# Values gathered in one tile and stored once per head, keys of two heads stored together, and projection weights split one row tile earlier

## The chip, the cores and the metric

The kernel runs on one core of a Trainium2 chip. The core has five engines with an instruction stream each: TensorE (PE in the profile, with its weight loads as PEld), VectorE (DVE), ScalarE (ACT), GpSimd (POOL) and SyncE (SP, which here only issues DMAs). Each stream runs in order; streams wait for each other through semaphores. DMAs move data between SBUF, where the engines work, and DRAM. The metric is the device time of one execution in microseconds; lower is better. The figure to compare is the median of several executions.

## The reference

```python
xn = layernorm(x)                                  # x: 1024 rows x 512
q = rmsnorm(xn @ Wq.T, q_norm_w)                   # 32 heads of 128
k = rmsnorm(xn @ Wk.T, k_norm_w)                   # 8 heads of 128
v = xn @ Wv.T                                      # 8 heads of 128
scores = q k^T / sqrt(128) + alibi bias, causal    # 4 query heads share one key/value head
s = (softmax(scores) @ v) @ Wo.T
g = silu(down(silu(xn @ gate) * (xn @ up)))        # weights dequantized from integers, width 1792
out = x + s * g
```

All inputs and the output are float32 (the quantized weights are integers).

## The kernel before

The work comes in four stages. First the layer norm, whose result is kept transposed as a high and a low float16 part (`xth`, `xtl`). Then the gate and up projections and the down projection of the feed-forward part, whose result is parked in DRAM (`gd`). Then the projections of queries, keys and values, which go through DRAM as well. Last the attention with its output projection, which ends with the output.

The change lies in the third stage and in the end of the second. There are 12 projections of 512 columns (line 618): in turn one of kind `kv` (keys and values of two heads, 256 + 256 columns) and two of kind `q` (four query heads each). Each is computed in 8 row tiles of 128 rows. A row tile is 12 matmuls of 512 columns (`mm3`: high by high, high by low, low by high, for four parts of the inner size) into one PSUM tile. The PSUM tiles take turns over two tags with two buffers each, so TensorE can be at most four row tiles ahead of the engines that empty them.

`Projection.tile` (line 532) issues a row tile's matmuls and the work that empties it. On ScalarE: a copy to `f` (542), squares with sums for the norm (544), and for `kv` the high part of the values (548). On VectorE for `kv`: the low part of the values (549). Both parts go to `v16`, a small tile with three buffers (546), and `store_values` (552) stores them one step later with two DMAs, one for each head.

The queries and keys are finished later, through a table of deferred work, `finishing`, which `finish_step` (448) runs once per row tile (`defer`, and `queue_half` at line 715). The steps are the inverse norm on VectorE (`inverse`) and GpSimd (`newton`), the multiplication on GpSimd (`normalize`), the high and low halves on VectorE (`halves`, 592), a DMA transpose (`transposed`, 606) one step after that and the store (`store`, 611) two steps after that. The finishing of a projection thus mostly falls into the next projection. While a `kv` projection runs, the finishing of a `q` projection goes on beside it.

The weights of projection k+1 are prepared during projection k by `prepare` (623), at given row tiles t: at t = 0 `squares` (471, sums of squares of the weight columns, on ScalarE), at 2 `norms` (483, a small matmul and scale factors on VectorE), at 3 `scale`, at 6 `factors`, and at 3 to 6 the split into high and low parts, `wh` on ScalarE (523) and `wl` on VectorE (524); for `kv` two head parts and then two value parts. The raw weights come by four DMAs in row tiles 0 to 3 of projection k-1 (line 966), into a pool of two buffers.

The order on every engine is the order in which the loop at lines 957 to 975 issues the work: in a row tile `prepare` for the next projection, the load for the one after that, the row tile itself, then the deferred work. All DMAs of the stage are issued by SP, in that order: weight loads (469), value stores (554), DMA transposes (608), query stores (613), key stores (616). Before the tenth projection the first keys, values and queries of the attention are loaded, and in the last two projections every second row tile also issues a step of the attention.

In DRAM the keys lie in one buffer per head, `kd` (124), row tile by row tile with 512 bytes per partition, and the values in one buffer per head, `vd` (125), partition by partition. `load_keys` (738) and `load_values` (742) bring a whole head back for the attention.

Of the kernel before, what the change touches and what calls it, by code (L numbers as in the profile page):

```python
# [12 lines left out]
F16 = mybir.dt.float16  # L13
# [8 lines left out]
P = 128  # L22
# [3 lines left out]
HKV = 8  # L26
NH = 4
HD = 128
FF = 1792
NI = FF // P  # L30
NT = S // P
# [39 lines left out]
def attention_gated_by_ffn_kernel(ctx, tc, x, gu_w, gu_z, gu_s, dn_w, dn_z, dn_s, wq, wkv, wo, qnw, knw, out):  # L71
    nc = tc.nc
    ve, se, ge, te, sp = nc.vector, nc.scalar, nc.gpsimd, nc.tensor, nc.sync

    const = ctx.enter_context(tc.tile_pool(name="const", bufs=1))
    dram = ctx.enter_context(tc.tile_pool(name="scratch", bufs=1, space=DRAM))
# [5 lines left out]
    def ps1(tag, name):  # L82
        return psum[0].tile([P, 512], F32, tag=tag, name=name)
# [22 lines left out]
    def mm3(ps, lhs, rhs, first, last):  # L106
        (lh, ll), (rh, rl) = lhs, rhs
        te.matmul(ps, lhsT=lh, rhs=rh, start=first, stop=False)  # L108
        te.matmul(ps, lhsT=lh, rhs=rl, start=False, stop=False)  # L109
        te.matmul(ps, lhsT=ll, rhs=rh, start=False, stop=last)  # L110
# [10 lines left out]
    eps = const.tile([P, 3 * HKV // 2, NH], F32, name="eps")  # L121
    gsT = const.tile([P, NI, 2, KT], F32, name="gsT")

    kd = [dram.tile([NT, P, 2 * HD], F16, name=f"kd{g}") for g in range(HKV)]
    vd = [dram.tile([P, NT, 2 * HD], F16, name=f"vd{g}") for g in range(HKV)]
    qd = [dram.tile([NT, P, 2 * NH * HD], F16, name=f"qd{g}") for g in range(HKV)]
    ald = [dram.tile([1, 2 * HD], F32, name=f"ald{i}") for i in range(HKV // 2)]
# [2 lines left out]
    left = ExitStack()  # L130
# [3 lines left out]
    wp = left.enter_context(tc.tile_pool(name="w", bufs=1))  # L134
# [264 lines left out]
    def dn_load(it):  # L399
        if it % 2 == 0:  # L400
            wi = gp.tile([P, 2, DM], I32, tag="wi", name=f"dni{it}", bufs=3)
            sp.dma_start(wi, dn_w[it * P : (it + 2) * P, :].rearrange("(t p) c -> p t c", p=P))
            dn_raw["pair"] = (wi, wi.bitcast(F32))
        zi = gp.tile([P, DM], I32, tag="dzi", name=f"dnz{it}")
        si = gp.tile([P, DM], F32, tag="dsi", name=f"dns{it}")
        sp.dma_start(zi, dn_z[it].partition_broadcast(P))
        sp.dma_start(si, dn_s[it].partition_broadcast(P))
        dn_raw[it] = tuple(w[:, it % 2, :] for w in dn_raw["pair"]) + (zi, si)

    def dn_dequant(it, engine=ge):  # L410
        wi, wf, zi, si = dn_raw[it]
        ve.tensor_tensor(wf, wi, zi, ALU.subtract)
        engine.tensor_tensor(wf, wf, si, ALU.mult)
# [40 lines left out]
    def defer(steps, f):  # L454
        finishing.setdefault(clock[0] + steps, []).append(f)
# [4 lines left out]
    class Projection:  # L460
# [71 lines left out]
        def tile(self, t):  # L532
            n, half, r = self.n, t // HT, t % HT
            if r == 0:
                self.f[half] = fq.tile([P, HT, n, HD], F32, tag="f", name=f"f_{self.name}_{half}", bufs=3)
                self.ss[half] = fq.tile([P, HT, n], F32, tag="ss", name=f"ss_{self.name}_{half}", bufs=3)
                self.jk = wp.tile([P, NH, HD], BF16, tag="jk", name=f"jk_{self.name}_{half}")
            ps = ps1("o" if t % 2 else "m", f"ps_{self.name}_{t}")
            rows = slice(t * P, (t + 1) * P)
            for j in range(KT):  # L540
                mm3(ps, (xth[:, j, rows], xtl[:, j, rows]), (self.wh[:, j, :], self.wl[:, j, :]), j == 0, j == KT - 1)
            se.copy(self.f[half][:, r], ps[:, : n * HD].rearrange("p (g d) -> p g d", g=n))
            for i in range(n):
                se.activation(self.jk[:, i], ps[:, i * HD : (i + 1) * HD], AF.Square, accum_out=self.ss[half][:, r, i : i + 1])
            if self.kind == "kv":
                v16 = wp.tile([P, 2, 2, HD], F16, tag="v16", name=f"v16_{self.i}_{t}", bufs=3)
                vp = ps[:, 256:512].rearrange("p (g d) -> p g d", g=2)
                se.copy(v16[:, :, 0, :], vp)
                ve.tensor_tensor(v16[:, :, 1, :], vp, v16[:, :, 0, :], ALU.subtract)
                defer(1, lambda: self.store_values(t, v16))  # L550

        def store_values(self, t, v16):
            for i in range(2):
                sp.dma_start(vd[2 * self.i + i][:, t, :], v16[:, i].rearrange("p a d -> p (a d)"))

        def inverse(self, half):

# [53 lines left out]
        def store(self, t, tr):  # L611
            if self.kind == "q":
                sp.dma_start(qd[self.i][t], tr.rearrange("p c t -> p (c t)"))
            else:
                for i in range(2):
                    sp.dma_start(kd[2 * self.i + i][t], tr[:, 2 * i : 2 * i + 2].rearrange("p c t -> p (c t)"))

    projections = []
    for pr in range(HKV // 2):
# [3 lines left out]
    def prepare(k, t):  # L623

        if k < len(projections):
            p = projections[k]
            if t == 0:
                p.squares()
            elif t == 2:
                p.norms()  # L630
            elif t == 3:
                p.scale()
            elif t == 6:
                p.factors()
            if 3 <= t < 3 + p.n:
                p.split_head(t - 3)
            elif p.kind == "kv" and 5 <= t < 7:
                p.split_values(t - 5)

    def down_begin():  # L640
        dn_split_w(0)
# [4 lines left out]
    for it in range(3, NI):  # L646
        if it < 3 + 2 * KT:
            projections[(it - 3) // KT].load((it - 3) % KT)
        last = it == NI - 1
        gu_unit(  # L650
            it,
            None,
            it + 1 if not last else None,
            meanwhile={NI - 2: lambda: dn_dequant(0, ve), NI - 1: down_begin}.get(it, lambda: None),
            total=not last,
        )
        if it == NI - 5:
            prepare(0, 0)
        if it == NI - 4:
            prepare(0, 2)  # L660
        if it == NI - 3:
            dn_load(0)
            dn_load(1)
        if last:
            dn_load(2)
            dn_split_h(0, 1)
# [3 lines left out]
    for it in range(NI):  # L670
        for tb in range(2):
            if it == 0:
                two = [pair(f"dn_ps{tb}_{i}") for i in range(2)]
                acc[tb] = [two[i // 2][:, i % 2, :] for i in range(4)]
            if tb == 0:
                if it + 2 < NI:
                    dn_dequant(it + 2)
                if it + 3 < NI:
                    dn_load(it + 3)
                if it + 1 < NI:  # L680
                    dn_split_w(it + 1)
            if it + 1 < NI:
                dn_split_h(it + 1, tb)
            wh, wl = dn_w_hl[it]
            hh, hl = dn_h_hl.pop((it, tb))
            for i in range(4):
                c = slice(i * P, i * P + P)
                mm3(acc[tb][i], (hh[:, c], hl[:, c]), (wh, wl), it == 0, it == NI - 1)
            if tb:
                if it in (1, 2):  # L690
                    gu_total((NI - 1, None), it - 1)
                elif it == 3:
                    gu_finish(0)
                elif it == 4:
                    gu_finish(1)
                elif it == 5:
                    norm_weights()
                elif it >= NI - 6:
                    prepare(0, 9 - NI + it)
            if it == NI - 1:  # L700
                for i in range(4):
                    go = h[:, i, tb * 512 : tb * 512 + 512]
                    se.activation(go, acc[tb][i], AF.Silu)
                    sp.dma_start(gd[tb * 4 + i], go)
    ffn.close()
    psum.append(ctx.enter_context(tc.tile_pool(name="psum", bufs=2, space=PSUM)))


    fq = ctx.enter_context(tc.tile_pool(name="finish", bufs=2, side="right"))
    ap1 = ctx.enter_context(tc.tile_pool(name="attn1", bufs=2, side="right"))  # L710
    nrel = ap1.tile([P, S], F32, name="nrel", bufs=1)
# [23 lines left out]
    kT, vT, qT, woh, wol = {}, {}, {}, {}, {}  # L735
    trel, pT, oT, wor = {}, {}, {}, {}

    def load_keys(g):
        kT[g] = ap1.tile([P, NT, 2, P], F16, tag="kT", name=f"kT{g}")
        sp.dma_start(kT[g].rearrange("p t a k -> p t (a k)"), kd[g].rearrange("t p c -> p t c"))  # L740

    def load_values(g):
        vT[g] = ap1.tile([P, NT, 2, HD], F16, tag="vT", name=f"vT{g}")
# [213 lines left out]
    for k, p in enumerate(projections):  # L957
        if k == len(projections) - 3:
            load_keys(0)
            load_values(0)  # L960
            load_queries(*blocks[0])
            relative(0)
        for t in range(NT):
            prepare(k + 1, t)
            if k + 2 < len(projections) and t < KT:
                projections[k + 2].load(t)
            if t == HT:
                p.undo()
            p.tile(t)
            finish_step()  # L970
            if t % HT == HT - 1:
                queue_half(p, t // HT)
            if k >= len(projections) - 2 and t % 2 == 0:
                step(early)
                early += 1
# [46 lines left out]
```

## Time and profile before

| what | value |
| --- | --- |
| median of 3 executions | 1104.58 us (1102.62 to 1104.69) |
| the profiled execution | 1104.1 us, span 1102.3 us |
| PE busy in the span | 1029.0 us (93%) |
| DVE, ACT, POOL busy | 885.0, 794.4, 392.9 us |
| projections of q, k, v | 221.00 to 504.00 us |
| DMA queue of SP | 196.93 MB, 81.5% of 16 engines |

The span is the time between the first and the last instruction of the program in the profiled execution. "Busy" is the time in which an engine executes an instruction; matmuls overlap, so a busy TensorE is not necessarily at its peak. An engine's idle time is put down to what ended it. The issue of a DMA is an instruction of SP; the transfer itself comes after it and is told as a time to landing. The granted clock is the share of TensorE's full clock that it ran at.

### The profile page before, as it was taken

The page shows a single profiled execution, that of the slowest core. Times are in us where ns is not written, and L with a number is a line of the kernel's source. Part 1 is how long each engine was busy: PE and PEld are TensorE (multiplying, and loading weights), DVE is VectorE, ACT ScalarE, POOL GpSimd, SP SyncE. Part 2 cuts the span into 40 slices and gives each one's busy share as a digit, 9 for nine tenths or more (in the row PEclk, how much of TensorE's full clock was granted, in tenths as well). Part 3 has the DMA queues.
Part 4 walks back from the last instruction along what each step waited for, and adds up shares of the span by engine and source line. Part 5 has one row for each costly group of instructions (what it writes and reads, how often), then busy time and mean ns, then how long its engine had stood idle before and what let it go on. Part 6 is the DMA issues. An engine that isn't in the chain of part 4 may idle for free.

```text
span 1102.3 us, 18743 instructions
## 1 busy us (share of the span) xinstructions
PE 1029.0 (93%) x5912; PEld 623.2 (57%) x5912; DVE 885.0 (80%) x1752; ACT 794.4 (72%) x2123; POOL 392.9 (36%) x545
## 2 busy tenths in 40 slices
PE   7899899999999899898899999999999999999996
PEld 5333368844434344344666666666666576676664
DVE  7888897537787776787789797898898887969984
ACT  5767543478678585787789687797896887868972
POOL 2565552136878678560202304014021030033122
PEclk8999999999999999899999999999999999999999
DMA  5123245246998979979989999999997997999995
GB/s 195 58 86 115 67 129 163 64 134 146 221 214 175 244 179 256 227 162 217 220 165 214 182 222 206 195 207 183 206 209 180 197 214 167 187 232 206 228 199 116
DMA packets 461633, 198.12 MB, mean 180 GB/s; under 512 B 395810, under 2 KB 421726, under 8 KB 461534
## 3 DMA queue, kind: packets, MB, share of 16 engines
q1 hardware_dynamic: 461534, 196.93, 81.5%
q8 instruction: 46, 0.75, 0.3%
q14 instruction: 53, 0.43, 0.1%
HBM read 71.03 MB, written 29.36 MB: 91 GB/s over the span
## 4 chain that ended last, share of the span: by engine, by line
PE 49%; DMA 16%; DVE 13%; ACT 10%; issue 6%; POOL 3%; SPq 1%; DVEq 0%; ACTq 0%; POOLq 0%
DMA pT<-p 13%; PE av L108 4%; PE s L108 3%; PE s L109 3%; PE s L110 3%; PE ps_q L109 3%; PE av L109 3%; PE av L110 3%; PE ps_q L110 3%; PE ps_q L108 3%; PE op L108 3%; PE op L110 3%; PE op L109 3%; ACT p L801 2%; PE dn_ps L110 2%
## 5 line engine op out<-in xcount | busy, mean ns | idle before, releaser
L810 DVE SCALAR_TENSOR_TENSOR p<-pf,row,p 128x1024 f16<-128x1024 f32 (+7 forms) x256 | 217.5, 849 | 71.8 <-ACT p L801 69.6
L801 ACT ACTIVATE p<-pf,row 128x1024 f16<-128x1024 f32 (+7 forms) x256 | 197.0, 770 | 67.1 <-DMA pT<-p 63.6
L791 ACT ACTIVATE pf<-pf,row 128x1024 f32<-128x1024 f32 (+7 forms) x256 | 196.9, 769 | 38.0 <-DVE row L790 36.4
L761 POOL TENSOR_TENSOR wol<-wor,woh 128x512 fp32r<-128x512 f32 x32 | 57.7, 1804 | 431.2 <-ACT woh L760 431.1
L790 DVE CUSTOM_DVE_ANT_0 pf<-s,trel,cs 128x1024 f32<-128x1024 f32 (+7 forms) x256 | 207.0, 809 | 4.4 <-PE s L110 3.9
L108 PE MATMUL av<-pT,vT 128*128 128x256 f16 (+1 forms) x640 | 171.6, 268 | 23.8 <-DMA pT<-p 23.1
L109 PE MATMUL av<-pT,vT 128*128 128x256 f16 (+1 forms) x640 | 169.2, 264 | 0.0
L110 PE MATMUL av<-pT,vT 128*128 128x256 f16 (+1 forms) x640 | 168.9, 264 | 0.0
L108 PE MATMUL s<-kT,qT 128*128 128x512 f16 (+3 forms) x384 | 125.4, 327 | 6.3 <-DVE row L790 6.2
L109 PE MATMUL s<-kT,qT 128*128 128x512 f16 (+3 forms) x384 | 125.3, 326 | 0.0
L110 PE MATMUL s<-kT,qT 128*128 128x512 f16 (+3 forms) x384 | 123.6, 326 | 0.0
L108 PE MATMUL op<-woh,oh 128*128 128x512 f32 x248 | 121.6, 490 | 0.0
L108 PEld LDWEIGHTS <-vT 128*128 128x128 f16 x640 | 62.3, 97 | 103.5 <-issue 80.7
L108 PE MATMUL ps_q<-wh_q,xth 128*128 128x512 f16 x256 | 98.9, 386 | 5.2 <-ACT wh_q L523 5.2
L109 PE MATMUL ps_q<-wl_q,xth 128*128 128x512 f16 x256 | 99.0, 387 | 5.0 <-DVE wl_q L524 5.0
L110 PE MATMUL ps_q<-wh_q,xtl 128*128 128x512 f16 x256 | 98.9, 386 | 0.0
L110 PE MATMUL op<-woh,ol 128*128 128x512 f32 x248 | 98.6, 398 | 0.0
L109 PE MATMUL op<-wol,oh 128*128 128x512 f32 x248 | 97.5, 393 | 0.6 <-POOL wol L761 0.6
L838 ACT ACTIVATE oh<-av,rv 128x256 fp32r<-128x256 f32 x128 | 59.3, 463 | 26.6 <-PE av L110 26.2
L590 POOL TENSOR_TENSOR f_q<-f_q,inv_q 128x512 f32<-128x512 f32 x64 | 71.5, 1137 | 1.4
L844 DVE SCALAR_TENSOR_TENSOR ol<-av,rv,oh 128x256 fp32r<-128x256 f32 x128 | 61.1, 477 | 13.6 <-ACT oh L838 13.5
L109 PEld LDWEIGHTS <-vT 128*128 128x128 f16 x640 | 63.7, 100 | 13.4 <-issue 3.7
(178 smaller groups left out, 2284.2 us busy)
## 6 DMA issues: line engine op xcount, KB each, us to landing
qd<-tr_q SPq DMA_DIRECT2D x64, 256.0 KB, 3.2
qT<-qd SPq DMA_DIRECT2D x32, 512.0 KB, 4.2
wq<-in_wq SPq DMA_DIRECT2D x32, 256.0 KB, 3.8
wor<-in_wo SPq DMA_DIRECT2D x32, 256.0 KB, 3.2
gui<-in_gu_w SPq DMA_DIRECT2D x13, 512.0 KB, 3.7
wkv<-in_wkv SPq DMA_DIRECT2D x16, 256.0 KB, 3.8
vd<-v SPq DMA_DIRECT2D x64, 64.0 KB, 2.7
kd<-tr_kv SPq DMA_DIRECT2D x64, 64.0 KB, 1.9
```

The costliest lines, as they stand in the source:

```text
L108: te.matmul(ps, lhsT=lh, rhs=rh, start=first, stop=False)
L109: te.matmul(ps, lhsT=lh, rhs=rl, start=False, stop=False)
L110: te.matmul(ps, lhsT=ll, rhs=rh, start=False, stop=last)
L590: ge.tensor_tensor(f, f, ib, ALU.mult)
L761: ge.tensor_tensor(wol[g, i], raw, woh[g, i].bitcast(F32), ALU.subtract)
L790: ve.tensor_tensor_reduce(p, ps, trel[g][:, S - w :], cs[:, hh : hh + 1], 3e38, ALU.add, ALU.min, least[:, c])
L791: se.activation(p, p, AF.Exp, bias=least[:, c], scale=-1.0, accum_out=total[:, c])
L801: se.activation(p16[u, qt][:, :, 0, :], pf[u, qt], AF.Copy, scale=scale[:, qt : qt + 1])
L810: ve.scalar_tensor_tensor(lo, p, scale, hi, ALU.mult, ALU.subtract)
L838: se.activation(oh, av_ps[u], AF.Copy, scale=rv[:, g : g + 1])
L844: ve.scalar_tensor_tensor(ol, av_ps.pop(u), rv[:, g : g + 1], oh.bitcast(F32), ALU.mult, ALU.subtract)
```

## The change

It has three parts. First, the values: the high and low parts of all 8 row tiles of a `kv` projection go to one tile `v16` (8 KB per partition, one buffer, in a pool of its own), and each head's values are stored with one DMA two steps after the last row tile, instead of one DMA per row tile and head. Second, the keys: two heads share one buffer in DRAM, laid out partition by partition, so that a row tile's keys of both heads are stored with one DMA, and a head's keys come back as one run of 4 KB per partition. Third, the preparation of the weights moves one row tile earlier: `squares` to the last row tile of the projection before, `norms`, `scale` and the split to row tiles 1, 2 and 2 to 5; `factors` stays. For the first projection, which is prepared during the feed-forward part, the split falls on the same places as before; the squares of the second move into the down projection.

```diff
-    kd = [dram.tile([NT, P, 2 * HD], F16, name=f"kd{g}") for g in range(HKV)]
+    kd = [dram.tile([P, 2, NT, 2 * HD], F16, name=f"kd{i}") for i in range(HKV // 2)]
...
             if self.kind == "kv":
-                v16 = wp.tile([P, 2, 2, HD], F16, tag="v16", name=f"v16_{self.i}_{t}", bufs=3)
+                if t == 0:
+                    self.v16 = vp16.tile([P, 2, NT, 2, HD], F16, tag="v16", name=f"v16_{self.i}")
+                v16 = self.v16[:, :, t]
                 vp = ps[:, 256:512].rearrange("p (g d) -> p g d", g=2)
                 se.copy(v16[:, :, 0, :], vp)
                 ve.tensor_tensor(v16[:, :, 1, :], vp, v16[:, :, 0, :], ALU.subtract)
-                defer(1, lambda: self.store_values(t, v16))
-
-        def store_values(self, t, v16):
+                if t == NT - 1:
+                    defer(2, self.store_values)
+
+        def store_values(self):
             for i in range(2):
-                sp.dma_start(vd[2 * self.i + i][:, t, :], v16[:, i].rearrange("p a d -> p (a d)"))
+                sp.dma_start(vd[2 * self.i + i], self.v16[:, i].rearrange("p t a d -> p t (a d)"))
...
             else:
-                for i in range(2):
-                    sp.dma_start(kd[2 * self.i + i][t], tr[:, 2 * i : 2 * i + 2].rearrange("p c t -> p (c t)"))
+                sp.dma_start(kd[self.i][:, :, t, :], tr.rearrange("p (g a) t -> p g (a t)", g=2))
...
             p = projections[k]
-            if t == 0:
+            if t == -1:
                 p.squares()
+            elif t == 1:
+                p.norms()
             elif t == 2:
-                p.norms()
-            elif t == 3:
                 p.scale()
             elif t == 6:
                 p.factors()
-            if 3 <= t < 3 + p.n:
-                p.split_head(t - 3)
-            elif p.kind == "kv" and 5 <= t < 7:
-                p.split_values(t - 5)
+            if 2 <= t < 2 + p.n:
+                p.split_head(t - 2)
+            elif p.kind == "kv" and 4 <= t < 6:
+                p.split_values(t - 4)
...
         if it == NI - 5:
-            prepare(0, 0)
+            prepare(0, -1)
         if it == NI - 4:
-            prepare(0, 2)
+            prepare(0, 1)
...
-                elif it >= NI - 6:
-                    prepare(0, 9 - NI + it)
+                elif NI - 6 <= it < NI - 1:
+                    prepare(0, 8 - NI + it)
+                if it == NI - 2:
+                    prepare(1, -1)
...
+    vp16 = left.enter_context(tc.tile_pool(name="values", bufs=1))
...
-        sp.dma_start(kT[g].rearrange("p t a k -> p t (a k)"), kd[g].rearrange("t p c -> p t c"))
+        sp.dma_start(kT[g].rearrange("p t a k -> p t (a k)"), kd[g // 2][:, g % 2])
...
             prepare(k + 1, t)
+            if t == NT - 1:
+                prepare(k + 2, -1)
```

## The prediction

> **What bounds the kernel now.** The page says PE 93% busy, so the question is where TensorE loses time, and in the stage that is changed. I read first a table of stretches, cut at the first matmul of each projection in the matmul records (projections counted from 0; 0, 3, 6 and 9 are `kv`). Columns: stretch, its length, busy time of PE, PEld, DVE, ACT, POOL, granted clock, DMA share, GB/s.
>
> ```profile
> 241.74:262.48 20.74, 20.74 (x98) 9.41 (x97) 13.10 (x39) 17.80 (x82) 10.56 (x31) 1.00 0.59 133
> 283.67:304.75 21.08, 20.90 (x98) 9.43 (x97) 15.38 (x33) 13.91 (x59) 16.91 (x34) 1.00 1.06 225
> 304.75:329.64 24.89, 22.58 (x97) 9.81 (x97) 20.57 (x49) 19.03 (x88) 18.46 (x44) 0.93 0.97 215
> 350.83:375.40 24.57, 20.90 (x98) 9.40 (x97) 17.15 (x35) 14.02 (x59) 17.44 (x37) 1.00 1.08 244
> 375.40:398.98 23.58, 22.39 (x98) 9.77 (x98) 18.88 (x45) 19.03 (x88) 17.71 (x43) 0.93 0.95 220
> 420.16:449.28 29.12, 23.60 (x98) 9.97 (x97) 16.77 (x35) 14.02 (x59) 19.84 (x40) 0.88 1.14 269
> 449.28:478.25 28.97, 27.44 (x121) 12.19 (x121) 23.68 (x52) 22.24 (x93) 18.17 (x46) 0.94 0.77 192
> 478.25:504.00 25.75, 25.75 (x122) 11.86 (x121) 23.37 (x37) 21.25 (x87) 12.59 (x22) 1.00 0.90 179
> ```
>
> An undisturbed projection takes 20.74 us, all of it PE (projection 1). The last, with four attention steps in it, takes 25.75 us, all PE. Projections 3, 4, 6, 7, 9 and 10 are longer: by 0.34, 4.15, 3.83, 2.84, 8.38 (each against 20.74) and 3.22 us (10 against 25.75). Together 22.8 us are lost, always in a `kv` projection with a finishing `q` beside it or in the `q` that follows. That is all the change can get back in this stage.
>
> What TensorE waits for, from the waits of PE, ACT and DVE between 221 and 504 us (total, times, longest):
>
> ```profile
> PE ps_q L108 <- ACT wh_q L523: 5.2, 3, 3.7
> PE ps_q L109 <- DVE wl_q L524: 5.0, 3, 2.3
> PE ps_kv L108 <- DVE v L549: 4.1, 1, 4.1
> ACT v L548 <- DMA vd<-v: 20.5, 10, 7.9
> DVE v L549 <- ACT v L548: 44.6, 18, 12.6
> ```
>
> The first three are 14.3 us of idle TensorE: split weights come late, and once a PSUM tile isn't emptied. The rest of the 22.8, some 8.5 us, is half-rate running after each stall: matmuls then follow each other at 0.43 instead of 0.21 us for about 3 us, and the clock column shows it (0.93, 0.93, 0.88, 0.94). Behind both kinds of lateness stands ScalarE, which waits 20.5 us for value stores to leave `v16`, whose three buffers are too few when a store is late. Why it is late shows in the chain before the first stall (start, length, what):
>
> ```profile
> 302.30 0.38 SPq L554
> ...
> 302.74 3.47 DMA vd<-v
> ...
> 306.64 0.75 DVE wl_q L524
> ...
> 307.43 0.38 PE ps_q L109
> ```
>
> and in SP's timeline of one row tile just before:
>
> ```profile
> 300.30 1.24 SPq L608 DMA_TRANSPOSE tr_q<-q  x1
> 301.64 0.57 SPq L613 DMA_DIRECT2D qd<-tr_q  x1
> 302.30 1.01 SPq L554 DMA_DIRECT2D vd<-v  x2
> 303.41 1.24 SPq L608 DMA_TRANSPOSE tr_q<-q  x1
> ```
>
> SP needs 3.11 us for this row tile; TensorE needs 20.74 / 8 = 2.59. By medians: transpose 1.29, query store 0.52, two value stores 2 x 0.43 = 0.86, together 2.67, and 0.57 more where a weight load falls in. Over 8 row tiles with four loads: 8 x 2.67 + 4 x 0.57 = 23.6 us against 20.74. SP is the bound of a `kv` projection.
>
> **What the Trainium skill says.** "Perfetto Trace Analysis", section "What 'DMA-bound' means": a kernel can be bound on the issuing engine's sequencer, whose slices are descriptor generation and not data movement, and larger descriptors help there. The trace agrees: 2.67 us of SP per row tile against 2.59. "DMA: Bandwidth & Descriptors", section "Rules for kernel authors": join small transfers, since small ones are mostly overhead. In SP's time the trace agrees: a 64 KB value store holds it 0.43 us, the 512 KB load of a head's values 0.57. "TensorE: Matmul & The Clock Gate", section "What's actually happening": an idle array falls to half clock, and it takes a busy window of about 3.4 us to get the full one back. The trace shows about 3 us at 0.43 us per matmul after each stall. "Perfetto Trace Analysis", section "DMA Instruction — HWDGE (DVE, Sync)": the profiled issue excludes the semaphore wait before it and the movement after it, so SP's sums here are a floor.
>
> **The change part by part.**
>
> *Values.* Each `kv` projection loses 16 stores (16 x 0.43 = 6.9 us of SP) and gets two of 512 KB, two row tiles into the next projection: 2 x 0.43 to 2 x 0.57 us of SP (the median of the store of before, and of the load of the same shape); I take 1.1. SP's need in a `kv` projection falls from 23.6 to 8 x 1.81 + 4 x 0.57 = 16.8 us. The next projection's SP has transposes and stores of keys, the lighter half, so the 1.1 us are hidden there; without cover they would cost just that, three times. ScalarE's 20.5 us of waits go, as no row tile of a `kv` projection reuses a buffer; the one tile is written again 16 row tiles after its store. Queued behind the first late copy (548) were the split (523), the next `f` copies and VectorE's line 549, and so the halves, the transposes and SP again: this loop is cut. ScalarE and VectorE do the same work as before.
>
> *Keys.* 16 stores per `kv` become 8 with twice the rows. A store of 128 KB by SP isn't shown; it lies between 0.43 (the 64 KB store) and 0.57 us (a 256 KB weight load), I take 0.52, as the query store. That saves 16 x 0.43 - 8 x 0.52 = 2.7 us of SP per `kv`, in `q` projections, where TensorE waits for nothing that SP delays: worth 0 here. The load of keys moves the same 512 KB in longer pieces; values, already in 4 KB runs, land in 4.7 us and keys in 4.5, so I expect nothing: 0, between -1 and +1 us over 8 loads.
>
> *Weights earlier.* No instruction is added or lost. The last split, behind which TensorE waits at a projection's start, is queued one row tile (2.59 us) earlier on ACT and DVE. The squares (four times 0.63 with 0.19 for the sum, some 3.2 us of ACT) go ahead of the emptying of row tile 7 instead of the next row tile 0; four PSUM tiles hide that as before. The small matmul of `norms` keeps its two tiles' distance from the squares. What is tighter is the raw weights: they must have landed one row tile earlier. In projection 9, the most crowded, the last load is issued at 441.94 and lands at 446.04; the emptying of row tile 6, after which ScalarE would reach the squares, begins at 449.13. So 3 us are left at the worst place; cost 0. In the down projection the 3.2 us of squares for the second projection come after ScalarE's last split there, beside TensorE's matmuls; cost 0, and at most the 3.2 us if ScalarE should be late for them.
>
> *What is late next.* Three deductions. (a) VectorE after projections 3 and 6: in 3 it waits for the first value copy until 289.69 and then needs about 2.1 us of instructions per row tile, more where they are drawn out by GpSimd (the query subtraction takes 0.69 or 1.41). By hand the last `wl` comes at about 302.7, wanted at 304.4. I deduct 0.5 us each, 1.0 in all (0 to 6). (b) Projection 9 also brings the attention's first 1.5 MB. It moved 269 GB/s x 29.12 us = 7.8 MB; without 1.0 MB of values 6.8 MB, which at that rate (the highest in the table) is 25.3 us against 20.74. Part can slip into projection 10 (192 GB/s), so of 4.6 us I deduct 2.5 (0 to 6). (c) In projections 10 and 11 the chain runs over ACT and DVE from 461.78 to 508.70, not over PE: they were late with TensorE, and might stay late when it isn't. Bounds 0 and the 3.2 us of projection 10; I deduct 2.0.
>
> Sum: 22.8 - 1.0 - 2.5 - 2.0 = 17.3 us. The attention starts when the projections end and its chain depends on nothing earlier, so the gain passes through whole. From the profiled 1104.1 us (span 1102.3 and 1.8 around it) that makes 1086.8; the median lies 0.5 above that execution, so 1087.3 us.
>
> **The rivals.**
>
> *Another engine or the DMAs take over in the `kv` projections.* For: DMA share is 1.06 to 1.14 there, VectorE 87% of 41.5 us in projections 3 and 4 taken at full speed. Against: SP's wait was first in each loop, and the share was lower than 1 in the projections next to them. Deductions at their upper ends, 6 + 6 + 3.2 = 15.2, leave 7.6 us: about 1097 us.
>
> *The change doesn't do what it says.* If slices of the one value tile were guarded as a whole, ScalarE would wait for VectorE in place of the DMA at each row tile, and stalls would only change their name: about 1104 us. Against: the row slices of `wh`, written and read alike by head, show no such wait.
>
> *Slower: the squares wait for the weights.* `norms`' matmul stands in TensorE's queue two row tiles after them, so lateness beyond the 3 us above goes to PE. It decides against the change from 22.8 / 10 = 2.3 us of stall in each of ten projections, thus a load 5.3 us later than in projection 9. Ten loads each 6.3 us later cost 10 x 3.3 = 33 us: 1104.6 - 22.8 + 33 = 1115 us. Against: SP, which issues the loads, is relieved of six us per `kv` projection.
>
> **How the numbers follow.** The relief as summed, with 13 to 24 us gained (1080.5 to 1091.5): 0.64. Another engine or the DMAs take over (1091.5 to 1101): 0.20. A larger gain, if the attention's start gets smoother too (to 1076): 0.03. Nothing changes (within 0.2%, 2.2 us, about what a measurement of this kernel can tell): 0.05. Slower: 0.08. So faster 0.87, same 0.05, slower 0.08. The range from 1079 to 1099 leaves out the two last, a tail of the second and part of the third: about 0.18.
>
> **What would show it.** Right: no wait of ACT's line 548 for a DMA of the values; projections 3, 4, 6 and 7 within 1 us of 20.74 and at clock 1.00; 9 below 25 us; SP's issues in a `kv` projection near 17 us; the stage from 221 to about 487. The attention from the stage's end to the end of the span as long as before (598.3 us). Wrong: waits of `ps_q` for `wh_q` or `wl_q` that remain, now behind POOL, the DMA transposes or `in_wq`; a matmul of `norms` that TensorE waits for; or an attention that is longer by what the projections saved.

## The result, and the profile after

The changed kernel takes 1093.99 us (median of four executions, 1091.06 to 1096.23) against 1104.63 us before: the ratio is 0.9895, with a 95% interval from 0.9855 to 0.9936. It is faster, by 10.6 us; 17.3 had been forecast. The ratio is an estimate from all executions and not the quotient of the two medians, which would be 0.9904. The profiled execution took 1093.67 us, its span is 1091.9.

The gain can be placed. The projections run from 220.77 to 492.03 us, 271.26 us instead of 283.00. The attention behind them takes 599.9 us instead of 598.3. Together with 0.2 us ahead of the projections that makes the 10.4 us between the spans.

The table of stretches of the changed kernel, cut as before at the first matmul of a projection (stretch, length, busy time of PE, PEld, DVE, ACT, POOL, granted clock, DMA share, GB/s):

```profile
283.44:304.19 20.75, 20.75 (x99) 9.39 (x98) 16.16 (x31) 15.07 (x65) 17.10 (x34) 1.00 1.05 237
304.19:325.88 21.69, 20.90 (x99) 9.38 (x97) 19.20 (x47) 16.77 (x82) 16.72 (x37) 1.00 0.90 233
...
347.06:368.60 21.54, 20.91 (x99) 9.43 (x98) 16.93 (x33) 14.06 (x62) 18.18 (x37) 1.00 1.10 245
368.60:392.36 23.76, 20.91 (x99) 9.43 (x98) 21.24 (x49) 18.80 (x90) 18.21 (x39) 1.00 0.98 244
...
413.54:435.08 21.54, 20.90 (x99) 9.42 (x97) 17.18 (x32) 13.15 (x57) 18.78 (x37) 1.00 1.06 273
435.08:466.29 31.21, 27.44 (x123) 12.20 (x121) 26.69 (x60) 22.57 (x97) 21.18 (x52) 0.95 0.95 233
```

These are projections 3, 4, 6, 7, 9 and 10. The sum of what all projections take beyond the undisturbed 20.74 (21.18 beside a `kv` being prepared, 25.74 for 10 and 11) is called the loss below: it was 22.8 us, it is 11.1. The half rate after a stall is almost gone in this profile: the clock is 1.00 everywhere but in projection 10. What the engines wait for now, in the same three views (total, times, longest), between 221 and 495 us:

```profile
PE ps_q L109 <- DVE wl_q L524: 7.4, 3, 3.8
PE n_ps L487 <- ACT sb_q L479: 1.3, 2, 0.6
...
ACT wh_q L523 <- DVE am_q L88: 16.6, 6, 5.5
...
DVE v L551 <- ACT v L550: 31.5, 15, 12.2
DVE q L605 <- POOL f_q L593: 21.0, 13, 2.9
```

No wait for a store of values is left. The splits that TensorE waits for are late on VectorE alone, and VectorE's waits for GpSimd, 11.8 us before, have become 21.0. SP's timeline at the same place as before shows what it was relieved of, two issues per row tile:

```profile
297.23 1.45 SPq L611 DMA_TRANSPOSE tr_q<-q  x1
298.83 0.49 SPq L616 DMA_DIRECT2D qd<-tr_q  x1
299.38 1.28 SPq L611 DMA_TRANSPOSE tr_q<-q  x1
```

From one transpose to the next, a row tile now takes SP 2.15 us (297.23 to 299.38), where it took 3.11. The chain before the largest of the new stalls but one runs over other engines (start, length, what):

```profile
366.57 0.23 POOL inv_q L587
...
366.86 1.05 POOL f_q L593
...
367.94 1.26 DVE q L605
...
369.22 1.41 DVE q L606
...
371.03 0.76 DVE wl_q L524
...
371.83 0.38 PE ps_q L109
```

GpSimd ends the inverse norm of a half projection (small instructions, one after another) and multiplies. VectorE then makes the halves of the queries, and only after that comes the split that TensorE has waited for since 369.0.

### The profile page after: what moved, and what is told of

Its sections match the earlier page's. It is cut to its first block, busy times and chain, and to the rows that moved or that the text cites. A ratio compares the mean times of both kernels' runs of the same rounds, so it can differ in the third digit from the quotient of the medians.

```text
span 1091.9 us, 18601 instructions
## 1 busy us (share of the span) xinstructions
PE 1023.7 (94%) x5912; PEld 620.8 (57%) x5912; DVE 890.6 (82%) x1752; ACT 790.8 (72%) x2123; POOL 396.4 (36%) x545
## 4 chain that ended last, share of the span: by engine, by line
PE 42%; DVE 19%; DMA 12%; ACT 11%; issue 8%; POOL 7%; SPq 1%; DVEq 0%; ACTq 0%; POOLq 0%
DMA pT<-p 11%; PE av L108 3%; PE s L108 3%; PE s L109 3%; PE s L110 3%; PE av L109 3%; PE av L110 3%; PE op L108 3%; PE op L110 3%; PE op L109 3%; DVE pf L795 3%; ACT p L806 2%; PE dn_ps L110 2%; PE dn_ps L109 2%; PE dn_ps L108 2%
## 5 line engine op out<-in xcount | busy, mean ns | idle before, releaser
L108 PE MATMUL av<-pT,vT 128*128 128x256 f16 (+1 forms) x640 | 171.1, 267 | 22.8 <-DMA pT<-p 22.5
```

## Experiments: which part of the change gained

The kernel before ran again beside each group of kernels. Its median was 1102.2 us beside the four of this section, 1101.5 us beside the first four of the next and 1105.7 us beside the last four. Each ratio is to the executions beside it, so kernels of different groups are compared by their ratios, not by their times. The diffs show the lines that matter; "..." stands for what is left out.

**Values alone.** Of the change only the one tile for the values and its stores.

```diff
-                v16 = wp.tile([P, 2, 2, HD], F16, tag="v16", name=f"v16_{self.i}_{t}", bufs=3)
+                if t == 0:
+                    self.v16 = vp16.tile([P, 2, NT, 2, HD], F16, tag="v16", name=f"v16_{self.i}")
+                v16 = self.v16[:, :, t]
...
```

> Of the change only the values (one tile, one store per head). If the value stores were the cause of the stalls, as the prediction has it, this alone gives nearly the whole gain: 1093 to 1097 us, no wait of the value copy on ScalarE for a DMA, and the stalls that remain are those of the changed kernel. If the earlier split is what helped, the time stays above 1100 us, because the split weights are late for another reason.

1091.94 us, ratio to the kernel before 0.9914 (0.9885 to 0.9942): the whole gain, as far as the intervals tell. The `kv` projections are undisturbed; the stalls fall on the queries after them. Its stretches for projections 3, 4, 6 and 7:

```profile
283.05:303.79 20.74, 20.74 (x98) 9.39 (x97) 15.08 (x31) 14.80 (x64) 16.89 (x34) 1.00 1.14 234
303.79:327.33 23.54, 20.91 (x99) 9.42 (x97) 20.81 (x50) 18.06 (x82) 18.54 (x41) 1.00 0.89 222
...
348.51:369.26 20.75, 20.75 (x99) 9.43 (x98) 15.87 (x31) 14.74 (x64) 17.68 (x35) 1.00 1.11 257
369.26:395.67 26.41, 22.59 (x99) 9.82 (x97) 22.03 (x53) 18.16 (x83) 18.86 (x45) 0.94 0.97 238
```

The loss is 14.1 us. In the three `kv` projections the DMA share is as high as before (1.14, 1.11 and 1.14), and they run undisturbed at it.

**Weights alone.**

```diff
-            if 3 <= t < 3 + p.n:
-                p.split_head(t - 3)
+            if 2 <= t < 2 + p.n:
+                p.split_head(t - 2)
...
```

> Of the change only the weights, prepared one row tile earlier. If the value stores are the cause, the loop of ScalarE, VectorE and SP stays as it was and the split is late with it: 1101 to 1107 us, and ScalarE still waits some 20 us for value stores. If a row tile of lead is what was missing, it covers most of the 3.7 and 2.3 us waits: below 1098 us.

1100.27 us, ratio 0.9986 (0.9974 to 0.9998), a gain of 1.5 us. The loss is 20.4 us, and ScalarE's wait is where it was:

```profile
ACT v L548 <- DMA vd<-v: 19.8, 9, 7.1
```

TensorE now also waits 4.9 us for the sums of the squares, which ScalarE makes late. So a row tile of lead helps little while ScalarE, which makes squares and splits, stands still for the stores.

**Values and keys**, without the weights.

```diff
-                for i in range(2):
-                    sp.dma_start(kd[2 * self.i + i][t], tr[:, 2 * i : 2 * i + 2].rearrange("p c t -> p (c t)"))
+                sp.dma_start(kd[self.i][:, :, t, :], tr.rearrange("p (g a) t -> p g (a t)", g=2))
...
```

> The change without the weights' shift. If joining the key stores is worth nothing, as predicted, this equals the kernel with the values alone within 2 us. Its distance to the whole change is what the shift of the weights adds on top: between 0 and 3 us by the prediction's view that the last split was late by one or two us; if the shift puts the scale factors behind work that waits for GpSimd, it adds nothing or costs something.

1093.35 us, ratio 0.9919 (0.9888 to 0.9950), loss 14.0 us: joining the key stores is worth nothing that can be seen. A joined store holds SP 0.545 us in the whole change (0.52 had been assumed), in projections where TensorE doesn't wait for SP.

**The kernel before with eight buffers for the values.** All stores stay.

```diff
-                v16 = wp.tile([P, 2, 2, HD], F16, tag="v16", name=f"v16_{self.i}_{t}", bufs=3)
+                v16 = vp16.tile([P, 2, 2, HD], F16, tag="v16", name=f"v16_{self.i}_{t}")
...
+    vp16 = left.enter_context(tc.tile_pool(name="values", bufs=8))
```

> The kernel before with eight buffers instead of three for the small value tile; all 128 stores of values and keys remain, and the weights keep their place. If the lack of buffers was the whole mechanism, it gains as much as the values alone: about 1094 us. If SP's issue rate is the bound of a kv projection (23.6 us of issues against 20.7 of matmuls), SP falls behind all the same, the query transposes come late, and VectorE waits for their buffers: 1099 to 1104 us, with SP's issues above 20 us in projections 3, 6 and 9.

1099.81 us, ratio 0.9973 (0.9960 to 0.9987). The loss is 19.3 us. Of the 8.7 us that the values alone take from the loss, the buffers, added first, account for 3.5 and the smaller number of issues for the other 5.2. SP is late as the second theory says, but one projection later than expected: its issues sum to 17.6, 19.6 and 18.7 us in projections 3, 6 and 9, and to 22.7, 21.8 and 32.0 in 4, 7 and 10, into which the backlog moves: of the 16 value stores of a `kv` projection, 8, 10 and 14 are issued only in the projection after it. VectorE and ScalarE then wait for what SP issues late:

```profile
DVE q L602 <- DMA tr_q<-q: 5.4, 4, 1.9
DVE k L602 <- DMA tr_q<-q: 4.6, 5, 1.6
```

```profile
ACT sq_q L476 <- DMA wq<-in_wq: 5.7, 1, 5.7
```

Slower transfers are not the cause, as far as the transposes show. From issue to landing the query transposes take 4.0 us by median here and 4.1 with the values alone, where nobody waits for them (between 283 and 470 us, in this order):

```profile
tr_q<-q SPq DMA_TRANSPOSE x43, 4.0
tr_q<-q SPq DMA_TRANSPOSE x43, 4.1
```

## Experiments: what holds the changed kernel

The theory after the result was that the finishing of queries, a loop between VectorE (inverse, halves) and GpSimd (Newton steps, multiplication), is what is left. The rivals were the DMAs, as deduction (b) has it, and the place of the scale factors in VectorE's queue.

**The changed kernel again**, for the comparison.

> The changed kernel as it is, beside the runs of its variants. 1091 to 1095 us. If the weights' shift is worth nothing on top of the values, as the kernels with the values alone and with values and keys suggest (1091.9 and 1093.4 us), it lies within 2 us of those, although its projections end some 3 us earlier in the profile.

1090.99 us, ratio 0.9905 (0.9876 to 0.9934), beside 0.9914 and 0.9919 of the kernels without the weights' shift. The loss is 11.1 us again, with other shares: 6.8 us in projections 6 and 7 and 3.3 in 9 and 10, where the first profile had 3.8 and 6.3. So the sum agrees from one profile to the other, but not the pair of projections in which the time goes. The 3 us by which the shift shortens the projections (271.26 against 274.2 us) can't be seen in the times.

**One Newton step instead of three.**

```diff
-        for i in range(3):
+        for i in range(2, 3):
             due((i + 1) // 2, 0, lambda i=i: p.newton(half, i == 2))
```

> The changed kernel with one Newton step of the inverse norms instead of three: 8 small GpSimd instructions less per half projection, some 3 us; this leaves out precision that the reference has. If what is left (11.0 us over undisturbed projections in the profile) comes from the loop in which VectorE's halves wait for GpSimd and GpSimd for VectorE's inverse, it falls to 5 us or less: 1085 to 1089 us. If the DMAs are what is left, nothing changes: 1091 to 1095 us.

This kernel leaves out precision that the reference has; it only shows what the two steps cost. 1084.32 us, ratio 0.9852 (0.9821 to 0.9882), 6.7 us below the changed kernel beside it; each of its six executions is faster than each of the other's six. The loss falls to 5.2 us, projections 3, 4, 6 and 7 are whole, and VectorE's waits for GpSimd, 21.0 us, are down to 0.7. Projections 6 and 7:

```profile
346.53:367.27 20.74, 20.74 (x98) 9.43 (x97) 17.23 (x36) 14.72 (x64) 12.90 (x18) 1.00 1.12 243
367.27:388.02 20.75, 20.75 (x99) 9.43 (x97) 17.59 (x40) 16.81 (x80) 12.02 (x24) 1.00 1.01 263
```

The DMA share and the rate are as high as ever (1.12; 263 GB/s) without a stall. So GpSimd's chain of small instructions held the changed kernel: 5.9 of its 11.1 us of loss go with it. The 5.2 us that stay lie in projections 8 to 10, where TensorE's one wait above 1 us, 2.3 us, is for the squares' sums.

**The attention's first loads one projection earlier.**

```diff
-        if k == len(projections) - 3:
+        if k == len(projections) - 4:
             load_keys(0)
             load_values(0)
             load_queries(*blocks[0])
+        if k == len(projections) - 3:
             relative(0)
```

> The changed kernel with the first 1.5 MB of keys, values and queries of the attention loaded one projection earlier. If the DMAs hold projections 9 and 10, as deduction (b) of the prediction has it, their loss (6.3 us) falls to that of 6 and 7 (3.8 us) or below: 1088 to 1091 us. If VectorE and GpSimd hold them, it stays at 6 us: 1091 to 1095 us.

1089.46 us, ratio 0.9894 (0.9866 to 0.9922), not to be told from the changed kernel. The loss is 11.0 us, as with the loads in projection 9. So these loads are not what holds the changed kernel.

**The scale factors ahead of the deferred work.**

```diff
-            elif t == 1:
-                p.norms()
...
             p.tile(t)
+            if t == 0 and k + 1 < len(projections):
+                projections[k + 1].norms()
             finish_step()
```

> The changed kernel with the weights' scale factors queued at the end of row tile 0, ahead of the deferred work of that row tile, instead of behind it. TensorE's order stays. If ScalarE's waits for the scale factors (16.6 us) stand in the way, because they are queued behind halves that wait for GpSimd, the splits come earlier and the stalls of projections 7 and 10 shrink: 1086 to 1090 us. If VectorE's rate alone is the bound, the last split is as late as before: 1091 to 1095 us.

1093.09 us, ratio 0.9921 (0.9900 to 0.9942): no gain, and the loss is 14.1 us. The scale factors do come earlier: in projection 6 they are ready 7.6 us after its start instead of 11.9. The last split is still 4.4 us late for projections 7 and 10 (3.2 and 4.1 in the changed kernel). Counted from the start of projection 6, the first split for projection 7 ends after 14.2 us instead of 15.0, but the last after 25.1 us instead of 24.7: halves still stand ahead of it in VectorE's queue. That the inverse norms come later, behind the scale factors, is seen only in part (1.7 us later in projection 3, 0.7 in 6, not in 9). The wait has changed its place:

```profile
ACT f_kv L542 <- POOL nwt_q L579: 16.4, 3, 6.1
```

**The kernel before with one Newton step.** The edit is that of the changed kernel with one step.

> The kernel before with one Newton step instead of three; it leaves out precision as the changed kernel with one step did. If the value stores bind first and the GpSimd loop only behind them, GpSimd's relief is hidden here: at most 2 us gained, 1099 to 1102 us. If the two costs simply add, it gains the same 6.7 us as in the changed kernel: about 1095 us.

1104.55 us, ratio 0.9998 (0.9981 to 1.0016): nothing, where the same edit gave 6.7 us in the changed kernel. ScalarE's wait for the stores stays:

```profile
ACT v L548 <- DMA vd<-v: 24.7, 13, 7.3
```

The two bounds lie behind each other: value stores first, GpSimd's chain behind them. (This kernel leaves out precision as well.)

**A shorter inverse norm of nearly the same precision.**

```diff
-            if last and self.kind == "q":
-                for i in range(NH):
-                    ...
-                    ge.tensor_scalar(wi, wi, -0.5 * c, 1.5 * c, ALU.mult, ALU.add)
+            if not last:
+                ge.tensor_scalar(w, w, -0.703952253, 1.681914, ALU.mult, ALU.add)
+            elif self.kind == "q":
+                ...
+                ge.tensor_tensor(w3, w3, half_c, ALU.mult)
+                ge.tensor_tensor(w3, w3, more_c, ALU.add)
...
-        for i in range(3):
-            due((i + 1) // 2, 0, lambda i=i: p.newton(half, i == 2))
+        for i in range(2):
+            due(i, 0, lambda i=i: p.newton(half, i == 1))
```

The first step has other constants, to go with another seed constant (0x5F1FFFF9); `half_c` and `more_c` hold -0.5 and 1.5 times the factors of the four heads.

> The changed kernel with a shorter inverse norm of nearly the same precision (7.6e-7): a better seed constant and two steps instead of three, and the last factors of the query heads from a constant tile. 9 small GpSimd instructions for a half of queries instead of 15, 8 for keys instead of 12. If the loop over GpSimd is what is left, most of the 6.7 us of the single step come: 1085 to 1089 us. If the single step gained by something else, about 1091 us.

1086.85 us, ratio 0.9830 (0.9808 to 0.9852), 18.9 us below the kernel before. Loss 6.6 us, projections 3, 4, 6 and 7 whole. What is left lies in 8 to 10, where raw weights land late for the squares, and TensorE's small matmul waits behind them:

```profile
PE n_ps L491 <- ACT sb_q L483: 2.9, 2, 2.7
...
ACT sq_q L480 <- DMA wq<-in_wq: 4.7, 2, 4.3
```

**The same with the attention's loads before projection 5 and its first bias before projection 0.**

```diff
-        if k == len(projections) - 3:
+        if k == 5:
             load_keys(0)
             load_values(0)
             load_queries(*blocks[0])
+        if k == 0:
             relative(0)
```

> The shorter inverse norm, with the attention's first loads moved from before projection 9 to before projection 5, and its first bias (1.3 us on GpSimd) to before projection 0. With one Newton step, 5.2 us of stalls were left, in projections 8 to 10, where raw weights landed late. If the 1.5 MB of loads cause that, 2 to 4 us more than with the shorter norm alone: 1082 to 1086 us; if not, the same as that.

1089.56 us, ratio 0.9853 (0.9826 to 0.9880): no further gain, a miss of the expectation. The loss is 6.4 us. In projections 9 and 10 it falls from 4.8 us to 0.7, but 4.0 us now lie in projection 6, where TensorE waits for the squares' sums of weights that landed late beside the moved loads:

```profile
PE n_ps L491 <- ACT sb_q L483: 2.2, 1, 2.2
```

The stall went where the loads went. With GpSimd relieved, the DMAs do hold a part of what is left, as far as one profile shows.

**The same without the weights' shift.**

> The same without the weights' shift: values, keys, shorter inverse norm, moved loads and bias. If the shift is worth nothing once GpSimd is relieved, because its squares then wait for raw weights, this is as fast as the kernel with the shift or faster, 1081 to 1086 us. If the row tile of lead counts, it is 2 to 4 us slower.

1085.45 us, ratio 0.9819 (0.9800 to 0.9839), the lowest ratio of all, though not to be told from that of the shorter inverse norm alone (0.9830). The loss is 4.9 us, and hardly any squares wait for weights (0.2 us). With GpSimd relieved, the shift is worth nothing; whether it costs something can't be told, as the interval of the kernel with it reaches 0.9826. This version, values and keys stored together, the weights at their old place, a shorter inverse norm and the moved loads, beats both the kernel before and the changed one (0.9895 and 0.9905, measured twice).

## Why the prediction was right or wrong, point by point

**What can be got back (22.8 us).** Right as a ceiling, and right in place: all that was gained in the projections comes from there, and the undisturbed projection still takes 20.74 us. The loss fell by 11.7 us.

**The value stores as the first cause.** Right, and shown by the parts: values alone 0.9914, weights alone 0.9986, keys nothing. Both halves of the mechanism count, SP's issues more than the buffers (5.2 and 3.5 us of the loss). SP's issues in projections 3, 6 and 9 were expected near 17 us; they sum to 14.3, 18.3 and 18.6, against 17.9, 20.6 and 24.9 before. The 23.6 us of the prediction are what a `kv` projection causes, not what falls into it: before, half of its 16 value stores were issued only in the projection after it. The Trainium skill, "Perfetto Trace Analysis", section "What 'DMA-bound' means", names the DMA engines and the issuing sequencer as different things that can bind. Here it was the sequencer, together with the few buffers: at the same DMA share (1.06 to 1.14 before, 1.11 to 1.14 with the values alone) the stalls of the `kv` projections are there or gone.

**Keys worth 0.** Right.

**Weights earlier.** The step that the split comes 2.59 us earlier was wrong in size. It ended, against the start of the projection that needs it, 1.1, 3.2 and 4.1 us late for projections 4, 7 and 10; in the kernel with values and keys alone 3.0, 4.1 and 4.2. The scale factors moved one row tile up in VectorE's queue, but stand there behind halves that wait for GpSimd: during projection 6 they are ready 11.9 us after its start with the shift and without it, and ScalarE's waits for them grew from 6.6 to 16.6 us. What an instruction gains by an earlier place in a queue is bounded by the one ahead of it. The cost of 0 for the raw weights holds nearly (one wait of 2.2 us, and TensorE waits 1.3 us for the squares' sums). The slower rival had the right place, but its size came to a few us: ScalarE waits 4.7 us for raw weights once the inverse norm is shorter.

**Deduction (a), VectorE after projections 3 and 6: 1.0 us.** This is the term that was mis-sized, and the step that failed in it was the working by hand from projection 3 alone, at nearly undisturbed durations. It had the last `wl` at about 302.7 us, before it is wanted; it came at 305.3, 1.1 us late. In 3 and 4 the loss is 0.95 us, but in 6 and 7 it is 3.8 us in one profile and 6.8 in the other. VectorE's finishing lags behind TensorE more in later rounds: the halves of a row tile end about 25 us after its matmuls start in projection 0, 29 to 31 in 2, and 31 to 34 in 5. That lag goes on into the next `kv` projection; I took VectorE to begin each one afresh. With one Newton step the lag in 5 is 27 to 29 us, and 6 and 7 lose nothing.

**Deduction (b), DMAs in projection 9: 2.5 us.** The size was too small (projections 9 and 10 together lose 6.3 us in the first profile and 3.3 in the second), and the cause was wrong: moving the 1.5 MB changed the loss from 11.1 to 11.0, while one Newton step in place of three more than halves it. What these loads cost shows only behind GpSimd's chain.

**Deduction (c), 2.0 us at the start of the attention.** Not shown. The attention took 1.6 us longer in this profile than before, but profiles of kernels with the same attention range from 593.9 us (loads earlier) to 600.1 us (the changed kernel again), in no order that follows the projections. The sentence that the gain passes through whole holds no closer than that.

**The rivals.** The time lies in the reach of the first rival, another engine that takes over in the `kv` projections, which had 0.20. It was the right one, with VectorE and GpSimd and not the DMAs as the ones that take over. It had been worked out at 1097 us; the measured 1094 lies between it and the forecast. The forecast's deductions came to 5.5 us against a loss of 11.1 that was left; that the time still lies in the range from 1079 to 1099 us is due to the width of the range and not to the deductions.

## What to carry to other kernels

Before a stall is counted as gain, ask what arrives late once it is gone, and follow that for several rounds of the loop: a lag that grows by a few us per round is hidden in the first one. An edit that gains nothing may stand behind another bound: one Newton step instead of three is worth nothing in the kernel before and 6.7 us after the change, so an idea that was dropped is worth a second try when the bound has moved. An instruction that is moved up in an in-order queue gets only as far as the wait ahead of it.

## What the runs showed of the hardware that was not expected

VectorE's halves of the queries take much longer while GpSimd multiplies. VectorE's timeline in the changed kernel:

```profile
367.94 1.25 DVE L605 CAST q<-f_q 128x512 f16<-128x512 f32 x1 [0.72 <-POOL f_q L593]
369.22 1.41 DVE L606 TENSOR_TENSOR q<-f_q,q 128x512 f16<-128x512 f32 x1
```

and GpSimd's beside it:

```profile
366.86 3.22 POOL L593 TENSOR_TENSOR f_q<-f_q,inv_q 128x512 f32<-128x512 f32 x3
```

Outside such stretches the same two take 0.42 and 0.69 us. In this profile none of the 42 subtractions that don't overlap one of these multiplications took more than 0.69 us; of the 22 that do, 19 took more than 1 us. The Trainium skill, "SBUF — State Buffer", section "Who interferes with whom", says that a VectorE instruction with two SBUF inputs contends with a GpSimd instruction that reads SBUF, and that casts can contend too, under conditions. The trace agrees, at 0.83 us for this cast and 0.72 for this subtraction. The prediction named the 0.69 and 1.41 but not what a GpSimd chain that is late does with them: it brings the multiplications and the halves together.

And a stall doesn't always cost the half rate. The same stall of the changed kernel, in the first profile and in the second, with the matmul that follows it:

```profile
371.83 0.38 PE L109 MATMUL ps_q<-wl_q,xth 128*128 128x512 f16 x1 [2.85 <-DVE wl_q L524]
372.04 0.38 PE L110 MATMUL ps_q<-wh_q,xtl 128*128 128x512 f16 x1
```

```profile
371.81 0.58 PE L109 MATMUL ps_q<-wl_q,xth 128*128 128x512 f16 x1 [2.84 <-DVE wl_q L524]
372.19 0.63 PE L110 MATMUL ps_q<-wh_q,xtl 128*128 128x512 f16 x1
```

In the first the matmuls go on some 0.21 us apart, in the second 0.38 and then 0.43. Projection 7 takes 23.76 us there and 26.69 here, which is the difference between 3.8 and 6.8 us above. In the kernel before, an idle time of 2.31 us at 305 to 307 us was followed by some 3 us at half rate. So the length of the stall alone doesn't decide it; what does is not shown. In the second profile VectorE's lag in projection 8 is 30 to 32 us instead of 32 to 35, and 9 and 10 lose less (3.3 instead of 6.3 us). This would fit VectorE catching up while TensorE is slow; no run tests it.
